# Rotating the first value tiles over three PSUM banks, moving the first head's mixes, and issuing two single residual loads ahead of large ones

## The chip, the cores and the metric

The kernel runs on one core of a Trainium2 chip. The metric is the device time of one execution in microseconds (us), as the median of several runs. Engines are named as the profile names them: PE is TensorE (PEld its weight loads), DVE is VectorE, ACT is ScalarE, POOL is GpSimd and SP is SyncE, which here only issues transfers. `L608` is line 608 of the kernel before.

## The reference

The input x has 2 sequences of 2048 positions with 256 features. First a recurrence is added to it, then an attention with experts (8 heads of width 64, 5 experts, 2 of them chosen for each position and head):

```python
x = x + rnn(layernorm(x))            # h = tanh(Wi x_t + bi + Wh h + bh), step after step
y = layernorm(x)
q, k = y @ Wq, y @ Wk                # per head, width 64
wv = topk_mask(y @ Ws, 2) * sigmoid(y @ Ws)      # gate of each expert
xv = einsum('btd,edk->btek', y, Wv)              # values of all 5 experts, no head in it
v  = einsum('bthe,btek->bhtk', wv, xv)           # a head's values: a weighted mix of experts
attn = softmax(q k^T / 8) v
mask_o = topk_mask(y @ Wd, 2)
x = x + einsum('bthe,bthk,ekd->btd', mask_o, attn, Wo)
```

The expert values xv are the same for all heads of a sequence. Only the mix v differs from head to head.

## The kernel before, in words

A first part, up to about 140 us, computes the recurrence in chunks and normalises. It isn't touched. It leaves x after the recurrence in DRAM as `x1d` (the residual that is added at the end) and its normalised transpose in SBUF as `xn2T`.

The attention works in 64 units: 16 heads (sequence by sequence, 8 each) by 4 blocks of 512 query positions. A unit has 4 steps, called T, and each step makes two score tiles: a tile has 128 key positions of two chunks by 512 queries (`scores`, L642). A tile goes through a pipeline that is LAG = 6 steps long:

- TensorE writes the scores in PSUM; ScalarE copies them to SBUF (`stage`, L654) and VectorE keeps a running maximum (`largest`, L664 to L670). Two score tiles fit in PSUM, so the second tile after waits for both.
- After a unit's eight tiles, TensorE transposes the maximum (`turn_max`, pm), VectorE reduces it (mq, L688), and TensorE spreads it over partitions (`spread_max`, pt, L697).
- The maximum is subtracted in SBUF (`subtract`, L710): on VectorE for a unit's first two tiles, on POOL for the other six. ScalarE takes the exponential (L713).
- TensorE multiplies with the head's values (`products`, L723, into o). POOL adds pairs of tiles with an accumulating DMA (`fold`, L735), and TensorE sums over the folded ones (`sums`, L744, into d).
- `take` (os, L759 and L760), `take_sums`, `weigh`, `masked` and `gather` bring a unit's output into `yd`, summed over heads; `turn_out` and `project_out` multiply with Wo (pz), add the residual z (L893) and store.

The values of the first sequence are made while the first head runs. `first_experts(c)` computes chunk c's values for all experts (tile pvf, 128 x 320 floats in PSUM, L581), ScalarE copies it to SBUF (xf, L608), and after each four chunks SyncE stores them for later heads. Tables of side work hold at which step it is issued: `first_experts(c)` stands behind step (c + 2) // 3, so chunk 0 at T=0, and chunks 13 to 15 at T=5. For the first head, `mix` multiplies four chunks by their gates on VectorE (wp, L624; L626), and `mix_sum` adds the five experts (L632). Within a step, `before` is issued ahead of the products, `between` after the tile copy and before the step's `largest`, and `behind` last.

[...] two buffers of a pool called misc (tiles pq, pk, pm, pt, wp, and others), one bank for o, one for d, and two score tiles of two banks each. In the drain, the scores' four banks serve other work.

The whole order is written out by hand (`with tc.manual_schedule()`): each engine executes its instructions in the order in which the program issues them, and waits at semaphores for what it needs. A transfer issued on SyncE waits in SyncE's queue as well.

After the last step, `drain()` finishes the last units: w, v and u are units 61, 62 and 63; tv and tu are the first tiles of v and u. The last outputs to be projected are numbered 0 to 15 in `outs`. The first four have a residual load each (`turn_out`, tag z, three buffers, 128 KB, L870), and the others come in blocks of four (`load_z`, 512 KB, L876). `fetch_y` (L810) reads a block of 640 KB from `yd`.

```python
z = yT_of.pop(("z", b, c), None)
if z is None:
    z = ap.tile([P, D], F32, tag="z", bufs=3, name=f"z{b}_{c}")
    nc.sync.dma_start(out=z, in_=x1d[c, :, b, :])
```

Of the kernel before, what the change touches and what calls it, by code (L numbers as in the profile page):

```python
# [8 lines left out]
F32 = mybir.dt.float32  # L9
# [5 lines left out]
P = 128  # L15
# [5 lines left out]
def pass_over(  # L21
# [17 lines left out]
    nc = tc.nc  # L39
    tc_pool, mark = tc.tile_pool, "s" if slow else ""  # L40

    def tile_pool(name, **kw):
        return tc_pool(name=name + mark, **kw)

    B, T, D = x.shape
    E, _, DH = Wv.shape
# [5 lines left out]
    NQ = T // QB  # L52
    QS = QB // P
# [17 lines left out]
    x1d = dram.tile([NCH, P, B, D], F32, name="x1d" + mark)  # L71
# [31 lines left out]
    for kc in range(KC):  # L103
        nc.sync.dma_start(
            out=wv[:, kc], in_=Wv[:, kc * P : (kc + 1) * P, :].rearrange("e p k -> p e k")
# [21 lines left out]
    def misc(shape, nm):  # L127
        return ps_m.tile(shape, F32, tag="m", name=nm)
# [148 lines left out]
    with tile_pool(name="prep", bufs=3) as pp, tile_pool(  # L277
        name="lna", bufs=3
    ) as lnp, tile_pool(name="ps_xi", bufs=3, space=PSUM) as ps_xi, tile_pool(
        name="ps_t", bufs=3, space=PSUM  # L280
# [286 lines left out]
    ap = ctx.enter_context(tile_pool(name="attn", bufs=2))  # L567
    four = ctx.enter_context(tile_pool(name="four", bufs=1))
    ps_o = ctx.enter_context(tile_pool(name="ps_o", bufs=1, space=PSUM))
# [7 lines left out]
    def by_quarters(dst, b, c, w):  # L577

        for kc in range(KC):
            for g in range(0, P, 32):  # L580
                nc.tensor.matmul(  # L581
                    dst[g : g + 32],
                    lhsT=xn2T[:, kc, b, c * P + g : c * P + g + 32],
                    rhs=w[:, kc],
                    start=kc == 0,
                    stop=kc == KC - 1,
                    tile_position=(0, g),
                )
# [9 lines left out]
    def first_experts(c):  # L598

        part = c // 4  # L600
        if c % 4 == 0:
            tag = ("y", "y", "xq", "pro")[part]
            xq_of[0, part] = four.tile([P, 4, DH, E], F32, tag=tag, bufs=1 + (tag == "y"), name=f"xf{part}")
        xq = xq_of[0, part]

        pv = ps_o.tile([P, E, DH], F32, tag="d", name=f"pvf{c}") if c % 2 else misc([P, E, DH], f"pvf{c}")
        by_quarters(pv.rearrange("p e k -> p (e k)"), 0, c, wv.rearrange("p c e k -> p c (e k)"))
        nc.scalar.copy(xq[:, c % 4], pv.rearrange("p e k -> p k e"))  # L608
        if c % 4 == 3:
            nc.sync.dma_start(out=xvd[0, part], in_=xq)  # L610
# [75 lines left out]
    def reduce_max(u):  # L686
        pm, mq = mx_of[u]
        nc.vector.tensor_reduce(mq, pm, AX.X, ALU.max)  # L688
# [23 lines left out]
    def exponential(t):  # L712
        nc.scalar.activation(ring[t], ring[t], AF.Exp)  # L713
# [91 lines left out]
    def fetch_y(u):  # L805

        i, n = units[u]
        b, _ = heads[i]
        y_of[b, n] = four.tile([P, QS, E, DH], F32, tag="y", bufs=2, name=f"y{b}_{n}")
        nc.sync.dma_start(out=y_of[b, n], in_=yd[b, n])  # L810
# [37 lines left out]
    yT_of = {"n": 0}  # L848
# [5 lines left out]
    def turn_out(b, c):  # L854
        yf = y_of[b, c // QS][:, c % QS].rearrange("p e k -> p (e k)")
        py = other(f"py{b}_{c}")[:, : len(o_chunks) * P] if spare else misc([P, len(o_chunks) * P], f"py{b}_{c}")
        py = py.rearrange("p (k n) -> p k n", n=P)
        for k, (r0, m) in enumerate(o_chunks):
            nc.tensor.transpose(py[0:m, k, :], yf[:, r0 : r0 + m], ident)
        yT = yT_all[yT_of["n"] % 2]  # L860
        yT_of["n"] += 1
        full = sum(m == P for _, m in o_chunks)
        nc.scalar.copy(yT[:, 0:full, :], py[:, 0:full, :])
        for k, (r0, m) in enumerate(o_chunks):
            if m < P:
                nc.scalar.copy(yT[0:m, k, :], py[0:m, k, :])
# [3 lines that stand above are left out]
            nc.sync.dma_start(out=z, in_=x1d[c, :, b, :])  # L870
        yT_of[b, c] = (yT, z)

    def load_z(b, n):

        z = ap.tile([P, QS, D], F32, tag="p1", bufs=RING[1], name=f"zz{b}_{n}")
        nc.sync.dma_start(out=z, in_=x1d[n * QS : (n + 1) * QS, :, b, :].rearrange("c p d -> p c d"))  # L876
        for s in range(QS):
            yT_of["z", b, n * QS + s] = z[:, s, :]
# [76 lines left out]
    before, between, first_behind, behind = {}, {}, {}, {}  # L955

    def at(table, T, f, *a):
        table.setdefault(T, []).append(lambda: f(*a))
# [9 lines left out]
    for i, (b, h) in enumerate(heads):  # L968
        T0 = i * H_T
        if i == 0:  # L970
            at(before, 0, keys, 0, 1)
            for c in range(NCH):
                at(behind, (c + 2) // 3, first_experts, c)
        else:

            at(before, T0 - 3 * U_T + 2, keys, i, 0)
            at(before, T0 - 2 * U_T + 2, queries, i, 0)
            at(before, T0 - U_T + 2, keys, i, 1)
        at(before, T0 + 2, queries, i, 1)
        for part in range(4):  # L980
            if i == 0:
                at(behind, (3, 5, 6, 7)[part], mix, i, part)
                at(behind, (3, 5, 6, 7)[part], mix_sum, i, part)
            else:
                T = T0 + U_T * (part - 2) + 2
                at(behind, T - 2, fetch, i, part)
                at(behind, T, mix, i, part)
                at(before, T + 1, mix_sum, i, part)
        if h == H - 3 and b + 1 < B:
            for c in range(NCH):  # L990
                T = T0 + c // 2 * U_T + 1
                at(before if c % 2 else behind, T + c % 2, experts, b + 1, c)
# [25 lines left out]
    for u, (i, n) in enumerate(units):  # L1018
        b, h = heads[i]
# [3 lines left out]
        outs = [(b, n * QS + s) for s in range(QS)]  # L1023
# [19 lines left out]
    def drain():  # L1043


        w, v, u = len(units) - 3, len(units) - 2, len(units) - 1
        tv, tu = HC * v, HC * u
        outs = [(B - 1, c) for c in range(NCH)]
        turned, projected = 2, 1

        def turn(n=1):
            nonlocal turned
            for _ in range(n):
                turn_out(*outs[turned])
                turned += 1

        def project(n=1):
            nonlocal projected
            for _ in range(n):
                project_out(*outs[projected])  # L1060
                projected += 1

        load_z(B - 1, NQ - 3)
        load_z(B - 1, NQ - 2)
        spread_max(v)
        turn_max(u)
        subtract(tv + 6, True)
        subtract(tv + 7)
        reduce_max(u)
        take_sums(w)  # L1070
        exponential(tv + 5)
        project()
        spread_max(u)
        products(tv + 4)
        products(tv + 5)
        fold(tv + 2)
        fold(tv + 4)
        exponential(tv + 6)
        exponential(tv + 7)
        subtract(tu, True)  # L1080
        close(w)
        gather(w)
        turn()
        exponential(tu)
        subtract(tu + 1, True)
        exponential(tu + 1)
        subtract(tu + 7)
        subtract(tu + 2, True)
        products(tv + 6)
        products(tv + 7)  # L1090
        fold(tv + 6)
        turn()
        fetch_y(v)
        project()
        load_z(B - 1, NQ - 1)
        take(v)
        sums(tv, tv + 2, True, False)
        exponential(tu + 2)
        subtract(tu + 3, True)
        exponential(tu + 3)  # L1100
        subtract(tu + 4, True)
        project()
        products(tu)
        products(tu + 1)
        turn()
        fold(tu)
        subtract(tu + 5, True)
        exponential(tu + 4)
        turn()
        project()  # L1110
        products(tu + 2)
        products(tu + 3)
        fold(tu + 2)
        sums(tv + 4, tv + 6, False, True)
        take_sums(v)
        exponential(tu + 5)
        subtract(tu + 6, True)
        turn()
        project()
        exponential(tu + 6)  # L1120
        products(tu + 4)
        products(tu + 5)
        exponential(tu + 7)
        turn()
        fetch_y(u)
        project()
        close(v)
        gather(v)
        products(tu + 6)
        products(tu + 7)  # L1130
        take(u)
        project()
        sums(tu, tu + 2, True, False)
        sums(tu + 4, tu + 5, False, False)
        sums(tu + 6, tu + 7, False, True)
        take_sums(u)
        turn()
        turn()
        project()
        turn()  # L1140
        project()
        turn()
        close_last(u, outs[-QS - 2 :])
# [117 lines left out]
```

## Time and profile before

| | us |
|---|---|
| median of 3 runs | 1560.38 (1559.92 to 1560.54) |
| profiled execution, its own time | 1562.38 |
| its span in the profile | 1560.5 |
| TensorE busy | 1513.2 |
| VectorE, ScalarE, POOL busy | 1300.0, 1245.4, 1287.0 |
| stretch of the first head, 143 to 192 | TensorE busy 41.97 of 49 |
| stretch of the drain, 1490 to 1561 | TensorE busy 59.62 of 71 |
| between them, 192 to 1490 | TensorE busy 1283.9 of 1298 |

The granted TensorE clock was 0.999 over the whole span and 0.96 in the last stretch. A row of an engine in order of time has the start, the duration, the operation with its line, output and inputs, how many instructions it joins, and in brackets how long the engine was idle before it and what ended that idle time. Matmuls overlap, so the duration of a group is less than the sum of its single matmuls.

### The profile page before, as it was taken

What the parts mean: (1) busy time and instruction counts of PE and PEld (TensorE: products, weight loads), DVE (VectorE), ACT (ScalarE), POOL (GpSimd) and SP (SyncE); (2) the same over time, 40 slices, a digit from 0 to 9 for tenths busy, and PEclk for the clock granted to TensorE, in tenths of its full rate; (3) what the DMA queues carried; (4) which work ended last, traced back from release to release, by engine and by line L of the source; (5) the groups of instructions that cost most, each with busy time, mean ns of one, the idle gap of its engine ahead of it and who ended that gap; (6) DMA issues with size and microseconds to landing.
All of it is one profiled execution on the core that took longest, in us unless ns stands there. A gap on an engine that the chain in (4) does not pass through costs nothing.

```text
span 1560.5 us, 41474 instructions
## 1 busy us (share of the span) xinstructions
PE 1513.2 (97%) x17582; PEld 534.4 (34%) x17582; DVE 1300.0 (83%) x1811; ACT 1245.4 (80%) x1617; POOL 1287.0 (82%) x855
## 2 busy tenths in 40 slices
PE   6999899999999999999999999999999999999988
PEld 5984222222233333333223332222222222222233
DVE  7474899999988877888987779999999999899873
ACT  4674688888888888888887778888888888888863
POOL 3154699999999987999997778899999999999970
PEclk9999999999999999999999999999999999999999
DMA  5021478888888887788786777888888888888963
GB/s 167 1 109 40 114 163 196 190 189 176 177 178 179 183 183 162 163 178 179 160 200 156 167 161 176 175 178 176 175 177 179 175 179 180 174 170 176 195 163 92
DMA packets 86821, 254.15 MB, mean 163 GB/s; under 512 B 11808, under 2 KB 31072, under 8 KB 86624
## 3 DMA queue, kind: packets, MB, share of 16 engines
q0 software_dynamic: 43488, 164.65, 57.9%
q1 hardware_dynamic: 41504, 86.13, 16.6%
q8 instruction: 140, 2.29, 0.6%
q10 hardware_dynamic: 1632, 0.61, 0.2%
q14 instruction: 57, 0.47, 0.1%
HBM read 59.46 MB, written 50.33 MB: 70 GB/s over the span
## 4 chain that ended last, share of the span: by engine, by line
PE 63%; DVE 19%; ACT 7%; issue 5%; DMA 3%; POOL 1%; ACTq 0%; SPq 0%; DVEq 0%; POOLq 0%
PE s L642 21%; PE o L723 17%; DVE m L664 11%; ACT p L654 5%; PE d L744 4%; DVE pro L789 3%; PE pq L166 3%; PE pk L147 3%; PE pz L885 2%; PE phb L368 2%; PE px L309 1%; PE pha L368 1%; DMA p<-p 1%; DMA z<-x1d 1%; ACT p L713 1%
## 5 line engine op out<-in xcount | busy, mean ns | idle before, releaser
L710 POOL TENSOR_TENSOR p<-p,top 128x1024 f32<-128x1024 f32 x378 | 1005.1, 2759 | 25.8 <-ACT top L703 25.5
L654 ACT COPY p<-s 128x1024 f32<-128x1024 f32 x512 | 511.5, 1012 | 139.6 <-issue 60.8
L713 ACT ACTIVATE p<-p 128x1024 f32<-128x1024 f32 x512 | 538.8, 1064 | 51.3 <-DVE p L710 42.7
L642 PE MATMUL s<-q,k 64*32 64x512 f32 x4096 | 501.6, 596 | 4.9 <-ACT p L654 2.5
L642 PE MATMUL s<-qs,k 64*32 64x512 f32 x4096 | 501.6, 596 | 3.5 <-ACT p L654 1.8
L723 PE MATMUL o<-p,v 128*32 128x512 f32 x4096 | 492.4, 598 | 5.1 <-DVE os L760 4.3
L664 DVE TENSOR_TENSOR m<-s,m 128x1024 f32<-128x1024 f32 x320 | 390.7, 1221 | 85.5 <-PE s L642 76.1
L735 POOL DMA_DIRECT2D p<-p x254 | 259.9, 1023 | 103.2 <-issue 43.7
L723 PEld LDWEIGHTS o<-p,v 128*32 128x32 f32 x4096 | 114.0, 109 | 301.5 <-issue 158.9
L642 PEld LDWEIGHTS s<-q,k 64*32 64x32 f32 x4096 | 100.5, 106 | 156.0 <-ACT p L654 60.3
L642 PEld LDWEIGHTS s<-qs,k 64*32 64x32 f32 x4096 | 100.4, 106 | 154.2 <-ACT p L654 58.1
L710 DVE TENSOR_TENSOR p<-p,pt 128x1024 f32<-128x1024 f32 x126 | 152.4, 1210 | 0.0
L744 PE MATMUL d<-p,ones 128*32 128x512 f32 x1032 | 136.3, 592 | 1.6 <-DMA p<-p 1.6
L664 DVE TENSOR_TENSOR m<-s,p 128x1024 f32<-128x1024 f32 x64 | 78.4, 1225 | 50.5 <-ACT p L654 49.6
L789 DVE TENSOR_TENSOR pro<-po,mr 128x1280 f32<-128x1280 f32 (+1 forms) x67 | 95.9, 1431 | 3.2 <-DVE mr L785 0.5
L626 DVE TENSOR_TENSOR xq<-xq,wp 128x1280 f32<-128x1280 f32 x60 | 89.2, 1487 | 2.1
L632 DVE TENSOR_REDUCE v<-xq 128x256 f32<-128x1280 f32 x60 | 88.5, 1475 | 0.0
L166 PE MATMUL pq<-xn2T,wq 128*32 128x512 f32 x512 | 62.2, 598 | 0.0
L147 PE MATMUL pk<-xn2T,wk 128*32 128x512 f32 x512 | 61.5, 598 | 0.0
L744 PEld LDWEIGHTS d<-p,ones 128*32 128x32 f32 x1032 | 34.0, 110 | 79.9 <-issue 76.0
L843 POOL DMA_DIRECT2D yd<-pro x48 | 60.1, 1252 | 0.0
L403 POOL TENSOR_TENSOR x<-x,hvb 128x512 f32<-128x512 f32 x14 | 17.8, 1275 | 45.8 <-ACT hs L376 34.2
(178 smaller groups left out, 1492.3 us busy)
## 6 DMA issues: line engine op xcount, KB each, us to landing
p<-p POOLq DMA_DIRECT2D x254, 512.0 KB, 5.4
xq<-xvd SPq DMA_DIRECT2D x60, 640.0 KB, 4.3
yd<-pro POOLq DMA_DIRECT2D x48, 640.0 KB, 6.5
qs<-q SPq DMA_DIRECT2D x64, 128.0 KB, 4.8
yd<-pro SPq DMA_DIRECT2D x8, 640.0 KB, 5.9
y<-yd SPq DMA_DIRECT2D x8, 640.0 KB, 8.2
x<-in_x SPq DMA_DIRECT2D x16, 256.0 KB, 5.8
x1d<-x SPq DMA_DIRECT2D x16, 256.0 KB, 2.0
```

Of the source, the lines that this page charges most:

```text
L147: nc.tensor.matmul(pk[at_col : at_col + 32], lhsT=wk[:, kc, h * DH + g : h * DH + g + 32], rhs=xc[:, kc, c0 // 2 : (c0 + HC) // 2, o, :], ...
L166: nc.tensor.matmul(pq[at_col : at_col + 32, :], lhsT=wq[:, kc, h * DH + g : h * DH + g + 32], rhs=xn2T[:, kc, b, n * QB : (n + 1) * QB], s ...
L626: nc.vector.tensor_tensor(xq, xq, wp.unsqueeze(2).to_broadcast([P, 4, DH, E]), ALU.mult)
L642: nc.tensor.matmul(ss[g : g + 32, o, :], lhsT=k_of[i][half, c, g : g + 32], rhs=q_of[i, n][o][half, :], start=True, stop=True, tile_positi ...
L654: nc.scalar.copy(p, ss)
L664: nc.vector.tensor_tensor(m, ss, ring[t - 1] if c == 1 else m, ALU.max)
L710: eng.tensor_tensor(p, p, top.unsqueeze(1).to_broadcast([P, 2, QB]), ALU.subtract)
L713: nc.scalar.activation(ring[t], ring[t], AF.Exp)
L723: nc.tensor.matmul(o_of[u][at_col : at_col + 32, :], lhsT=v_of[i][:, 2 * c + o, g : g + 32], rhs=ring[t][:, o, :], start=c == 0, stop=c == ...
L735: nc.gpsimd.dma_start(out=ring[t], in_=ring.pop(t + 1), accum_op=ALU.add)
L744: nc.tensor.matmul(den_of[u][32 * g : 32 * (g + 1), :], lhsT=ones32, rhs=ring[(t, t1)[g // 2]][:, g % 2, :], start=first, stop=last, tile_ ...
L789: nc.vector.tensor_tensor(dst, po[:, s : s + n, 0:DH].unsqueeze(2).to_broadcast([P, n, E, DH]), mr[:, s : s + n].unsqueeze(3).to_broadcast ...
```

## The change

It has three parts, and none adds or removes an instruction.

1. `first_experts`: the PSUM bank of pvf c. Before, odd c used the bank tagged d and even c a misc buffer. After, c mod 3 chooses: 0 misc, 1 bank o, 2 bank d.
2. First head: `mix` and `mix_sum` of the four parts stood together behind T = 3, 5, 6, 7. After, the mixes are issued behind T=2, between at T=4, and behind T=5 and T=6; the sums behind T=2, between at T=4, behind T=6, and between at T=8.
3. Drain: a new helper `load_z1` issues a single residual load. The loads of outputs 2 and 3 (z2, z3) come at the beginning of the drain, ahead of `load_z` of block 1 (zz1); before, they were issued by their `turn_out`, behind zz1 and zz2. `load_z` of block 2 (zz2) takes the place that block 3 (zz3) had, and block 3's comes after `fetch_y(u)`.

```diff
--- before.py
+++ after.py
@@ -603,7 +603,8 @@
             xq_of[0, part] = four.tile([P, 4, DH, E], F32, tag=tag, bufs=1 + (tag == "y"), name=f"xf{part}")
         xq = xq_of[0, part]
 
-        pv = ps_o.tile([P, E, DH], F32, tag="d", name=f"pvf{c}") if c % 2 else misc([P, E, DH], f"pvf{c}")
+        tag = (None, "o", "d")[c % 3]
+        pv = ps_o.tile([P, E, DH], F32, tag=tag, name=f"pvf{c}") if tag else misc([P, E, DH], f"pvf{c}")
         by_quarters(pv.rearrange("p e k -> p (e k)"), 0, c, wv.rearrange("p c e k -> p c (e k)"))
         nc.scalar.copy(xq[:, c % 4], pv.rearrange("p e k -> p k e"))
         if c % 4 == 3:
@@ -870,6 +871,10 @@
             nc.sync.dma_start(out=z, in_=x1d[c, :, b, :])
         yT_of[b, c] = (yT, z)
 
+    def load_z1(b, c):
+        yT_of["z", b, c] = ap.tile([P, D], F32, tag="z", bufs=3, name=f"z{b}_{c}")
+        nc.sync.dma_start(out=yT_of["z", b, c], in_=x1d[c, :, b, :])
+
     def load_z(b, n):
 
         z = ap.tile([P, QS, D], F32, tag="p1", bufs=RING[1], name=f"zz{b}_{n}")
@@ -979,8 +984,8 @@
         at(before, T0 + 2, queries, i, 1)
         for part in range(4):
             if i == 0:
-                at(behind, (3, 5, 6, 7)[part], mix, i, part)
-                at(behind, (3, 5, 6, 7)[part], mix_sum, i, part)
+                at(between if part == 1 else behind, (2, 4, 5, 6)[part], mix, i, part)
+                at(between if part % 2 else behind, (2, 4, 6, 8)[part], mix_sum, i, part)
             else:
                 T = T0 + U_T * (part - 2) + 2
                 at(behind, T - 2, fetch, i, part)
@@ -1060,8 +1065,9 @@
                 project_out(*outs[projected])
                 projected += 1
 
+        for o in outs[2:QS]:
+            load_z1(*o)
         load_z(B - 1, NQ - 3)
-        load_z(B - 1, NQ - 2)
         spread_max(v)
         turn_max(u)
         subtract(tv + 6, True)
@@ -1092,7 +1098,7 @@
         turn()
         fetch_y(v)
         project()
-        load_z(B - 1, NQ - 1)
+        load_z(B - 1, NQ - 2)
         take(v)
         sums(tv, tv + 2, True, False)
         exponential(tu + 2)
@@ -1123,6 +1129,7 @@
         exponential(tu + 7)
         turn()
         fetch_y(u)
+        load_z(B - 1, NQ - 1)
         project()
         close(v)
         gather(v)
```

## The prediction

> **What bounds the kernel now.** I read the page's busy shares first, then the chain that ended last, then each engine in order of time in the two stretches that the change touches.
>
> ```profile
> PE 1513.2 (97%) x17582; PEld 534.4 (34%) x17582; DVE 1300.0 (83%) x1811; ACT 1245.4 (80%) x1617; POOL 1287.0 (82%) x855
> ...
> PE 63%; DVE 19%; ACT 7%; issue 5%; DMA 3%; POOL 1%; ACTq 0%; SPq 0%; DVEq 0%; POOLq 0%
> ```
>
> TensorE is busy 97% of the span, so a gain can come only from its idle time. In the 50 us in which the first head starts, TensorE's records in order of time show it (start, duration, work, and in brackets the idle time before it and its releaser):
>
> ```profile
> 146.45 3.44 PE L581 MATMUL pvf<-wv,xn2T 128*32 128x320 f32 x48 [1.08 <-ACT q L176]
> ...
> 154.53 1.28 PE L581 MATMUL pvf<-wv,xn2T 128*32 128x320 f32 x16 [0.47 <-ACT xf L608]
> ...
> 159.15 0.62 PE L697 MATMUL pt<-ident,mq 128*128 128x128 f32 x4 [0.88 <-DVE mq L688]
> ...
> 168.93 1.28 PE L581 MATMUL pvf<-wv,xn2T 128*32 128x320 f32 x16 [1.63 <-ACT xf L608]
> ...
> 180.70 0.63 PE L642 MATMUL s<-q,k 64*32 64x512 f32 x4 [1.30 <-ACT p L654]
> ...
> 183.18 0.63 PE L683 MATMUL pm<-ident,mm 128*128 128x128 f32 x4 [0.53 <-DVE wp L624]
> ...
> 186.82 0.65 PE L697 MATMUL pt<-ident,mq 128*128 128x128 f32 x4 [1.16 <-DVE mq L688]
> ```
>
> Those seven idles sum to 7.05 us. Three are a value tile that waits for a PSUM bank; four go back to VectorE. VectorE in order of time, just ahead of the pt at 159.15:
>
> ```profile
> 155.13 0.17 DVE L624 COPY wp<-gates_all 128x20 f32<-128x20 f32 x1
> 155.34 1.49 DVE L626 TENSOR_TENSOR xf<-xf,wp 128x1280 f32<-128x1280 f32 x1
> 156.86 1.49 DVE L632 TENSOR_REDUCE v<-xf 128x256 f32<-128x1280 f32 x1
> 158.31 0.69 DVE L688 TENSOR_REDUCE mq<-pm 128x4 f32<-128x512 f32 x1
> ```
>
> A mix (0.17 + 1.49) and its sum (1.49) stand ahead of the row maximum mq. In the drain, the chain that ended last leaves TensorE:
>
> ```profile
> 1506.06 10.57 DMA z<-x1d
> ...
> 1516.72 0.25 DVE z L893
> 1516.97 0.20 issue
> 1517.18 0.70 DVE os L760
> 1517.88 0.14 issue
> 1518.02 3.27 PE o L723 x16
> ```
>
> A 128 KB residual, issued at 1506.06, lands 10.57 us later. VectorE's add waits for it and the take of the outputs (os) is behind the add on the same engine; TensorE's products behind that start after 2.03 us of idle and take 3.27 us, where the same 16 take 1.90 elsewhere. One more idle of TensorE nearby:
>
> ```profile
> 1513.63 0.62 PE L744 MATMUL d<-p,ones 128*32 128x512 f32 x2 [1.08 <-DMA p<-p]
> ```
>
> It is the fold of POOL issued at 1504.00, landed 9.6 us later. After 1518 TensorE has no gap over 0.2 us until 1554.3, and the execution ends at 1560.5.
>
> [...] the trace's 0.47 and 1.63 us are tile c waiting for tile c-2's copy out of one. [...] z1 (128 KB), issued at 1501.82 ahead of the large ones, landed in 2.6 us, z2 behind them in 10.6. [...] The 3.27 against 1.90 us fits a lowered clock[...].
>
> **Part 1, banks of the value tiles.** No work is added. Tile c goes to misc, o, d by c mod 3, so it needs tile c-3's copy and not c-2's; bank o is free until products(0), which come after pvf15. The waits at 146.45 (pvf4 in misc behind the query copy), 154.53 and 168.93 go: 1.08 + 0.47 + 1.63 = 3.18. A copy takes 0.43 and three tiles take 3.37 us of TensorE, so three banks cover it. The misc ring still holds pm, pt, wp; its two buffers now have fewer users.
>
> **Part 2, mix steps.** Same operations: four mixes and sums, 4 x 3.15 us of VectorE. Moved where VectorE idles (before 151.88 it had been idle 3.96, before 165.13 4.99). My walk, each instruction at the latest of its inputs:
> - Mix 0 with sum runs 147.95-151.15, delaying the maximum m7 by 0.5; tile s8 needs the copy of s7 (ends 153.41) at 153.92: margin 0.5.
> - Scores of T=4 start 153.92 (155.74 before); pt 157.2 (159.15), no mix ahead of mq now.
> - Mix 1 with sum, before T=4's maximum m9, 157.2-160.35: m9's end moves to 161.6, s11 needs its bank at 162.05: margin 0.45.
> - T=6's scores 166.37 (170.15): 3.8 gained. T=7's 171.95 (175.60).
> - VectorE is then full from 163.1 to 178.2, as it was from 165.13 to 187.9. That sets m15 at 174.85, its copy at 177.1, and s16 at 177.15 (180.70): 1.45 us of idle stays. Mix 3's sum, now before T=8's maximum, leaves mq1 earlier: pt1 at 181.45 (186.82), 0.85 idle between pm and pt1.
> - The stretch ends at 186.7 instead of 191.9: 5.2.
>
> Check: TensorE's work between 143.45 and 191.9 is 40.9 (pq 1.85, 12 value tiles at 1.12, seven pairs of scores at 1.88, pk 1.85, four pairs of products at 1.85, d 0.86, four transposes 2.3), so 7.5 is idle; 2.3 of it stays.
>
> POOL limits this. It is busy without a gap from 175.46, where its first fold waits for products(0,1), and that moves by 3.7 only. Its subtracts end 0.26-0.97 us ahead of the exponentials of the first three units (record by record, L710's end to L713's start), and a late exponential has 1.3 us of other products on TensorE as cover. So at least 3.7 + 0.26 = 4.0, at most 5.3; I take 4.9. From there units last 20.3 us in a loop of TensorE, ScalarE and VectorE, with 1.13 us of slack on POOL: the gain is carried along. The upper end needs the cover to hold, the lower end is the bare sum.
>
> **Part 3, drain.** No DMA is added; six change place. SyncE's order becomes z1, z2, z3, zz1, out z1, y2, out z2, zz2, out z3, two outs, y3, zz3. [...] z3 waits for out z0 (issued 1501.43, landed +2.7); zz1 stands behind it. z2 is issued about 1502.6 and lands, at 2.6-4.0 like its neighbours, about 1506; at its old 10.6 it would be 1513.2. Needed: 1512.11, when VectorE has done its pair of subtracts. z3 (issued from 1504.1, needed 1516.0) and zz1 (from about 1505, needed about 1519) have over 11 us. The later loads stay covered: VectorE first added zz2 at 1541.16 and POOL y2 at 1535.09; less the gain, 1536 and 1530, over 15 us from issue; zz3 and y3 come after these. With the add at 1512.11, os is 1512.98-1513.67. TensorE ahead of it still waits for the fold of 1504.00. I put its landing at 1512.6 instead of 1513.6, since one of the two 512 KB loads issued just before it has gone; the d and pz behind it then end about 1514.9 (2.36 after the landing, as before), and products(tu) run 1514.9-1516.85, where they ended at 1521.28. That is 4.4: 2.03 idle, 1.35 of slow clock, 1.0 of the fold's wait.
>
> What is late next: the last fold of unit tv. POOL issues it at 1515.13, behind gather(w) and a subtract that the change doesn't touch; it landed in 5.8 us, and zz2, issued about 1513 now, shares the engines. Estimate 6.5, so 1521.6. Its matmuls d, the second half of which reads it, began at 1525.61 and would begin at 1521.2, that half at 1521.7: nothing lost, gain 4.4. If it takes 9.7 us, as the one issued 1506.74 did, it lands at 1524.8 and the gain is 1.4. Best, with no fold late and os as the limit: 5.3.
>
> **Sum.** 4.9 + 4.4 = 9.3 us. The profiled execution took 1562.38, its span 1560.5; the median of runs, 1560.38, is equal to the span, so I take it as base: 1551.1 us.
>
> **Rivals.**
> - *POOL holds the head.* Cover on TensorE is not there: 4.0 from the head, 8.4 in all, 1552.0; with part of the drain lost 1553. For: POOL's slack of 0.26 us at unit 2. Chance 0.2.
> - *The fold takes z2's place.* zz2 slows the fold: 4.9 + 1.4, 1554.1. For: two of six folds took over 9 us while 512 and 640 KB loads ran; against: now only zz2 comes close to this one. Chance 0.17.
> - *The mixes re-stall.* Margins of 0.45-0.5 us fail at s8, s11 or s14: head 3, in all 7.4, 1553.0. Chance 0.12.
> - *Slower: cadence.* The head leaves POOL late, the loop settles on POOL's pace instead. Decides if POOL stays more than 2.4 us (slack 1.13 + cover 1.3) behind; 0.2 us on each of 55 units is 11 us: 1562. Against: POOL's lag is 1.5 by the walk, and units 28 and 29 came with 0.03 us of slack without a longer cadence. Chance 0.04.
> - *Nothing moves in the drain*: z2's 10.6 us was traffic, not its place. Even so it lands at 1513.2, costing at most 1.1: 1552.2. Chance 0.03.
>
> **How the numbers follow.** The forecast has 0.44; the rivals' cases 0.56. A measurement here tells 0.2%, 3.1 us, from no change. Range: below, both ends best (5.3 + 5.3): 1549.8, less 0.8 for a walk's error, 1549.0; above, 1556.0, fold and head both poor (3 + 1.4). All but the slower rival (0.04) and stacked losses (0.04, counted as same) are faster: 0.92, 0.04, 0.04.
>
> **What would show it.** Right: no wait for xf at L581; mq without a mix ahead; an idle of 1.4 at s16; the add z without a DMA wait, the 16 products after it near 1.9 us. Wrong: an ACT wait on POOL in units 1 to 3, a fold from 1515 landing after 9 us, a new idle at s8 or s11, or units other than 20.3 us apart.

## The result, and the profile after

The changed kernel took 1554.93 us in the median of 6 runs (1551.82 to 1556.47), the kernel before 1560.73 (1559.92 to 1561.83). The ratio is 0.9955, 95% interval 0.9945 to 0.9965: 7.0 us faster by the ratio, 5.8 by the medians. The forecast was 1551.1 in a range of 1549.0 to 1556.0. So the time lies in the range and the sign was right, but the likeliest sum, 9.3 us, was too large: by a third against the ratio, by more than half against the medians. The profiled execution took 1555.04 us, its span 1553.2.

First the busy shares of the changed kernel; the chain that ended last has the same shares as before.

```profile
PE 1512.4 (97%) x17582; PEld 533.9 (34%) x17582; DVE 1300.0 (84%) x1811; ACT 1246.0 (80%) x1617; POOL 1287.7 (83%) x855
...
PE 63%; DVE 19%; ACT 7%; issue 5%; DMA 3%; POOL 1%; ACTq 0%; SPq 0%; DVEq 0%; POOLq 0%
```

No work has gone; the span lost idle time. TensorE in order of time, 143 to 192 us, now has only two idles with a releaser, where there were seven (line numbers are one higher than before):

```profile
157.03 0.65 PE L698 MATMUL pt<-ident,mq 128*128 128x128 f32 x4 [0.79 <-DVE mq L689]
...
176.96 0.63 PE L643 MATMUL s<-q,k 64*32 64x512 f32 x4 [1.49 <-ACT p L655]
```

No value tile waits for a copy any more in this stretch. VectorE in order of time shows the moved mix: the row maximum mq comes first now, and the mix stands behind it.

```profile
156.29 0.69 DVE L689 TENSOR_REDUCE mq<-pm 128x4 f32<-128x512 f32 x1 [1.86 <-PE pm L684]
156.89 0.17 DVE L625 COPY wp<-gates_all 128x20 f32<-128x20 f32 x1
157.10 1.49 DVE L627 TENSOR_TENSOR xf<-xf,wp 128x1280 f32<-128x1280 f32 x1
158.62 1.49 DVE L633 TENSOR_REDUCE v<-xf 128x256 f32<-128x1280 f32 x1
```

In the drain, VectorE's add of z2 (at 1507.37) follows its subtracts with no wait. Two rows of TensorE and the chain that ended last show what is waited for now:

```profile
1508.62 0.62 PE L745 MATMUL d<-p,ones 128*32 128x512 f32 x2 [0.72 <-DMA p<-p]
...
1518.03 1.05 PE L745 MATMUL d<-p,ones 128*32 128x512 f32 x4 [0.30 <-DMA p<-p]
```

```profile
1499.35 9.22 DMA p<-p
...
1508.62 0.49 PE d L745
...
1510.32 0.19 PE o L724
1510.51 7.48 DMA p<-p
...
1518.03 1.05 PE d L745 x4
```

A fold took the residual's place in the chain, and then a later one, the fold of tile 6 of unit v (the last that v's sums read).

To say where the time went without the noise of the rest, I divided every profile at four events: the first copy of a score tile by ScalarE (L654), the first exponential of units 4 and 20, and the last copy of a score tile. "Head" is the time from the first copy to unit 4, "to 20" from the first copy to unit 20, "drain" from the start of the last copy to the end of the span, all in us. The last row is of runs that are told below.

| profile | first copy at | head | to 20 | drain | span |
|---|---|---|---|---|---|
| before | 129.00 | 124.65 | 461.16 | 61.46 | 1560.5 |
| changed | 128.93 | 120.40 | 456.75 | 58.86 | 1553.2 |
| gain | | 4.25 | 4.41 | 2.60 | 7.3 |
| before, five more with the old drain | 128.7 to 130.5 | | | 58.53 to 59.44 | |

### The profile page after: what moved, and what is told of

It is laid out like the page before. It is cut to its first block, busy times and chain, and to the rows that moved or that the text cites. A ratio compares the mean times of both kernels' runs of the same rounds, so it can differ in the third digit from the quotient of the medians.

```text
span 1553.2 us, 41472 instructions
## 1 busy us (share of the span) xinstructions
PE 1512.4 (97%) x17582; PEld 533.9 (34%) x17582; DVE 1300.0 (84%) x1811; ACT 1246.0 (80%) x1617; POOL 1287.7 (83%) x855
## 4 chain that ended last, share of the span: by engine, by line
PE 63%; DVE 19%; ACT 7%; issue 5%; DMA 3%; POOL 1%; ACTq 0%; SPq 0%; DVEq 0%; POOLq 0%
PE s L643 21%; PE o L724 17%; DVE m L665 11%; ACT p L655 5%; PE d L745 4%; DVE pro L790 4%; PE pq L166 3%; PE pk L147 3%; DMA p<-p 2%; PE pz L890 2%; PE phb L368 2%; PE px L309 1%; PE pha L368 1%; PE pv L581 1%; ACT p L714 1%
## 5 line engine op out<-in xcount | busy, mean ns | idle before, releaser
L736 POOL DMA_DIRECT2D p<-p x254 | 263.1, 1036 | 95.8 <-issue 42.3
L403 POOL TENSOR_TENSOR x<-x,hvb 128x512 f32<-128x512 f32 x14 | 17.9, 1276 | 45.8 <-ACT hs L376 34.2
```

The lines of the kernel that those rows point to most:

```text
L736: nc.gpsimd.dma_start(out=ring[t], in_=ring.pop(t + 1), accum_op=ALU.add)
```

## The experiments

Times are medians; a ratio is to the kernel before on the same chip, with its 95% interval.

**The head and the drain alone, and each kernel once more.** The first kernel leaves out the drain's edit (and its helper):

```diff
-        for o in outs[2:QS]:
-            load_z1(*o)
         load_z(B - 1, NQ - 3)
+        load_z(B - 1, NQ - 2)
...
-        load_z(B - 1, NQ - 2)
+        load_z(B - 1, NQ - 1)
...
-        load_z(B - 1, NQ - 1)
```

> Parts 1 and 2 alone (banks and mix steps), the drain as before. Theory A (the head gives the 4.65 us by which every late unit is shifted in the profile, and the drain's share in the medians is small): 4.6 us faster, about 1556.1. Rival B (the profile-to-profile reading is the true one; of a median gain of 5.8 the drain gives 2.9): 2.9 us faster, about 1557.8.

Measured: 1557.57 us, ratio 0.9967 (0.9956 to 0.9978), 5.2 us, near theory A's 4.6; B's 2.9 lies outside the interval (3.4 to 6.9). Head 120.32, drain 58.95. The second leaves out the head's edits (banks and mix steps as before):

```diff
-        tag = (None, "o", "d")[c % 3]
-        pv = ps_o.tile([P, E, DH], F32, tag=tag, name=f"pvf{c}") if tag else misc([P, E, DH], f"pvf{c}")
+        pv = ps_o.tile([P, E, DH], F32, tag="d", name=f"pvf{c}") if c % 2 else misc([P, E, DH], f"pvf{c}")
...
-                at(between if part == 1 else behind, (2, 4, 5, 6)[part], mix, i, part)
-                at(between if part % 2 else behind, (2, 4, 6, 8)[part], mix_sum, i, part)
+                at(behind, (3, 5, 6, 7)[part], mix, i, part)
+                at(behind, (3, 5, 6, 7)[part], mix_sum, i, part)
```

> Part 3 alone (the order of the residual loads), the head as before. Theory A: about 1.2 us faster, 1559.5, since the profiled execution of the kernel before was 2 us above the median of its runs and so its drain was a slow one. Rival B: 2.9 us faster, 1557.8. My prediction's own number was 4.4: 1556.3.

Measured: 1560.22 us, ratio 0.9986 (0.9979 to 0.9992), 2.2 us. Head 124.71, drain 58.42. The other two are the two kernels with no edit.

> The kernel before, unchanged, to have a second profiled execution of it and the spread between two sets of its runs. Theory A: the residual z2 lands sooner than the 10.6 us of the first profile, and the stretch from 1490 to the end is 1 to 2 us shorter. Rival B: it lands after 10 us again and the products behind it wait 2 us. Ratio 1.000 within 0.001.

Measured: 1561.47 us, ratio 0.9998 (0.9990 to 1.0006).

> The changed kernel, unchanged, for a second profiled execution and more runs. Both theories: about 5.8 us faster, 1554.9. Theory A: head again 4.65; the drain's end is set by the folds that the sums of unit tv read, and their landing (9.2 and 7.5 us in the first profile) differs by 1 us or more between the two executions, which makes its runs spread over 4.6 us. Rival: the folds land alike, and the spread comes from the middle units.

Measured: 1555.57 us, ratio 0.9961 (0.9949 to 0.9973).

The head's 5.2 and the drain's 2.2 add up to about the whole (7.0 by the ratio); 2.2 lies between the numbers of theories A and B, and its interval (1.2 to 3.3) reaches to both. My own 4.4 is outside. The second profile of the kernel before says why. TensorE in order of time there:

```profile
1517.90 1.92 PE L723 MATMUL o<-p,v 128*32 128x512 f32 x16 [1.92 <-DVE os L760]
1519.76 0.87 PE L859 MATMUL py<-ident,y 128*128 128x128 f32 x6
```

Theory A expected z2 to land sooner. It didn't: z2 was issued at 1506.32 and took 10.20 us, and the products had 1.92 us of idle ahead of them as before. But they took 1.92 us, not 3.27, and the six transposes 0.87, not 1.17. The drain was 59.44, 2.02 us shorter. A window laid over both profiles around these products (start and end of the window, its length, busy time of TensorE, its weight loads, VectorE, ScalarE and POOL, granted clock, DMA share, GB/s) has the clock. The profile I predicted from:

```profile
1518.00:1522.00 4.00, 3.98 (x20) 1.44 (x21) 3.72 (x4) 1.06 (x1) 0.86 (x1) 0.57 0.98 263
```

and the second one of the same kernel:

```profile
1517.00:1521.00 4.00, 2.91 (x26) 1.26 (x30) 3.94 (x6) 1.66 (x4) 0.86 (x1) 1.00 1.01 226
```

The clock fell to 0.57 in one and stayed at 1.00 in the other. Six profiles in all have the old drain, with idles of 1.9 to 2.0 us at this place; only the first one slowed. So the idle is regular, and the slow clock was seen in one of six. What the runs show of it stands in the last section.

The second profile of the changed kernel has a drain of 56.88 against 58.86. There the fold that the first d reads took 7.95 us instead of 9.22, and that of tile 6 5.83 instead of 7.48, and no fold is in the chain that ended last. Even so, the second half of the next d began only when the fold of tile 6 had landed, and d took 2.00 us instead of 1.04.

**Banks alone, mixes alone.** The first takes the changed line for `pv` only, the second the two lines with `mix` and `mix_sum` only (the diff above, read the other way).

> Part 1 alone (three banks for the value tiles), mixes and drain as before. Stretch from ScalarE's first copy of a score tile to the first exponential of unit 4: 124.66 us in both profiles of the kernel before, 120.42 with parts 1 and 2. Theory: the two bank waits ahead of VectorE's full stretch (1.08 + 0.47) are gained, the third (1.63) is not, since VectorE, full from there to 187.9, sets the later steps: 123.1, 1.5 us faster, about 1560.5. Rival: all three are gained, 121.5, 3.2 us.

Measured: 1559.65 us, ratio 0.9990 (0.9982 to 0.9998). Head 123.47: 1.2 us, near the theory's 1.5. The copies are no longer waited for, and VectorE, with its mixes at the old steps, sets the time: TensorE waits 1.60 us for mq ahead of pt, and 1.79 at s16.

> Part 2 alone (the first head's mixes at their new steps), banks and drain as before. Theory: the same stretch is 122.0, 2.7 us shorter, so that parts 1 and 2 add up to the 4.25 seen: of the bank waits that come back (3.18), 1.6 is hidden by VectorE's later limit. About 1559.3. Rival: the bank waits all come back in full and it is 123.6, 1.1 us shorter.

Measured: 1560.95 us, ratio 0.9998 (0.9990 to 1.0007). Head 125.23, which is 0.6 longer than before (0.3 at unit 20). Both expectations fell: neither had a new wait. TensorE in order of time has one in its second row:

```profile
158.78 0.65 PE L697 MATMUL pt<-ident,mq 128*128 128x128 f32 x4 [0.79 <-DVE mq L688]
160.44 3.44 PE L581 MATMUL pvf<-wv,xn2T 128*32 128x320 f32 x48 [1.02 <-DVE xf L626]
...
169.67 1.28 PE L581 MATMUL pvf<-wv,xn2T 128*32 128x320 f32 x16 [1.62 <-ACT xf L608]
```

VectorE there, ahead of 160.44:

```profile
158.64 0.17 DVE L624 COPY wp<-gates_all 128x20 f32<-128x20 f32 x1
158.90 1.49 DVE L626 TENSOR_TENSOR xf<-xf,wp 128x1280 f32<-128x1280 f32 x1
```

A mix puts its gates (wp) in a misc buffer, and holds it until the multiply ends. Moved to T=4, mix 1 holds the buffer that the next even value tile (pvf10) is to have. A second new wait comes in unit 1, where VectorE's `weigh` (mr) needs the mask of the output experts (`gates_all`, L254), which POOL works out beside its folds and subtracts:

```profile
208.48 0.18 DVE L785 TENSOR_TENSOR mr<-po,gates_all 128x20 f32<-128x20 f32 x1 [1.97 <-POOL gates_all L254]
```

In the kernel before, this mask was ready 0.3 us ahead of need:

```profile
208.22 0.18 DVE L785 TENSOR_TENSOR mr<-po,gates_all 128x20 f32<-128x20 f32 x1
```

The move is only harmless if the value tiles are elsewhere. To test that, the next kernel keeps the moved mixes and takes the value tiles out of misc, but with two banks:

```diff
-        pv = ps_o.tile([P, E, DH], F32, tag="d", name=f"pvf{c}") if c % 2 else misc([P, E, DH], f"pvf{c}")
+        pv = ps_o.tile([P, E, DH], F32, tag="d" if c % 2 else "o", name=f"pvf{c}")
```

> Part 2 (mix steps) with the value tiles in two banks and none in misc: even ones in bank o, odd ones in d; drain as before. From the first copy of a score tile to the first exponential of unit 4 the profiles had 124.7 us before, 125.2 with part 2 alone, 120.4 with parts 1 and 2. Theory (half of what part 2 lost is that a value tile in misc waits for pq and for a mix's gates wp, which VectorE holds until its multiply ends): the two misc waits, 1.07 and 1.02, go, the two for bank d (0.47, 1.62) stay: 123.1. Rival (only the depth of the rotation counts; with two banks tile c waits for tile c-2 everywhere): 124.5 or more, new waits for xf at even tiles.

Measured: 1559.85 us, ratio 0.9993 (0.9983 to 1.0002). Head 123.20, the theory's number. TensorE's rows:

```profile
153.53 1.28 PE L581 MATMUL pvf<-wv,xn2T 128*32 128x320 f32 x16 [0.68 <-ACT xf L608]
158.06 0.65 PE L697 MATMUL pt<-ident,mq 128*128 128x128 f32 x4 [0.79 <-DVE mq L688]
167.87 1.28 PE L581 MATMUL pvf<-wv,xn2T 128*32 128x320 f32 x16 [1.62 <-ACT xf L608]
```

Both misc waits are gone and both waits for a copy two tiles back stay. So of the 4.8 us between mixes alone (125.23) and mixes with three banks (120.40), leaving misc gives 2.0 and the third bank 2.8. The parts don't add: 1.2 and -0.6 alone, 4.25 together.

The profiles show where the gain goes. All times in this table are us after the first copy of a score tile; the last column is how long VectorE waits for the mask in unit 1:

| profile | first d | POOL's first fold | mask ready | unit 4 (head) | wait |
|---|---|---|---|---|---|
| before | 62.03 | 45.88 | 78.90 | 124.65 | none |
| banks alone | 60.81 | 42.84 | 77.67 | 123.47 | none |
| mixes alone | 60.72 | 46.90 | 79.73 | 125.23 | 1.97 |
| mixes, two banks | 58.73 | 44.91 | 77.73 | 123.20 | 1.69 |
| changed | 56.74 | 42.03 | 74.90 | 120.40 | 1.11 |

With the mixes alone, TensorE reaches the first d 1.3 us earlier, with the banks alone 1.2. But with the mixes alone POOL's first fold, which stands behind the first products, comes 1.0 later, the mask comes late with it, and unit 1 takes the gain back. In the three kernels with moved mixes the head follows the mask, and the mask follows POOL's first fold. That is read from traces; no run moved POOL's work alone.

**Which part of the drain's edit.** Here z2 and z3 stay ahead, and zz2 and zz3 go back to their old places:

```diff
         load_z(B - 1, NQ - 3)
+        load_z(B - 1, NQ - 2)
...
-        load_z(B - 1, NQ - 2)
+        load_z(B - 1, NQ - 1)
...
-        load_z(B - 1, NQ - 1)
```

> The changed kernel with zz2 and zz3 back at their old places, so that of part 3 only z2 and z3 ahead of zz1 is left. Theory (z2's landing was the wait, and zz2's place matters little): from ScalarE's last copy of a score tile to the end 57.0 to 58.5, no wait of VectorE's add on z2; the fold issued 5.0 us after that copy lands 9 us later or more, as zz2 runs beside it again, and d waits about 1 us for it; the fold of tile 6 lands in 5.5. Median as the changed kernel, 1555. Rival (part 3's gain is zz2's move): 59 or more, 1557.

Measured: 1555.89 us, ratio 0.9968 (0.9957 to 0.9980): nearly the ratio of the head alone (0.9967), and 1.5 us above the changed kernel on the same chip (below), though the two intervals overlap. The drain was 61.18. VectorE's add didn't wait for z2, but:

```profile
1514.55 1.90 PE L724 MATMUL o<-p,v 128*32 128x512 f32 x16
1516.26 1.03 PE L745 MATMUL d<-p,ones 128*32 128x512 f32 x4
1519.83 1.32 PE L745 MATMUL d<-p,ones 128*32 128x512 f32 x4 [2.54 <-DMA p<-p]
...
1521.91 2.46 PE L890 MATMUL pz<-wo,yT 128*32 128x256 f32 x24
```

The fold took 8.56 us, the wait reached 2.54, and the clock fell again (0.66 from 1520 to 1525 us; pz 2.46 instead of 1.50). My theory had this fold at 5.5 us and fell. This execution took 1558.14 us, the slowest of its eight and 2.25 above their median, so 61.18 isn't the drain of a usual run. What the profile does show is a way to lose: as soon as the outs are not held up by z2, SyncE comes sooner to the large load queued behind them. zz3 was issued 13.9 us after the last copy of a score tile, 18.6 in the first profile of the kernel before, and so it runs beside the fold, which is issued 16.2 us after that copy. The changed kernel has a large load at this very place too, zz2, and TensorE is idle for only 0.30 us there. What is more here is the early zz2, which was in flight until 17.9 us after that copy. So zz2's move is likely to be needed, but that isn't shown: the medians don't decide it.

**Can the fold's wait be taken away?** In the first of three versions both sums (d) are issued later, in the second zz1, y2 and zz2:

```diff
-        sums(tv, tv + 2, True, False)
...
-        sums(tv + 4, tv + 6, False, True)
-        take_sums(v)
         exponential(tu + 5)
         subtract(tu + 6, True)
         turn()
         project()
+        sums(tv, tv + 2, True, False)
+        sums(tv + 4, tv + 6, False, True)
+        take_sums(v)
```

> The changed kernel with both sums of unit tv's folds (d) and the take of them moved behind the second next output's projection, so that no fold is waited for where TensorE has other work. From ScalarE's last copy of a score tile to the end the profiles had 58.9, 56.9 and 58.4 us with the new drain, 61.5, 59.4 and 59.0 with the old one. Theory A (the landing of the folds now sets the drain's length and its spread): 55.5 to 56.5, 1.5 us faster than the changed kernel in the median, about 1553.5, no idle of TensorE before d. Rival: the work after it waits for the later d (close of v), and nothing is gained: 58, 1555.3.

Measured: 1553.75 us (1552.26 to 1554.19), ratio 0.9951 (0.9939 to 0.9964), drain 56.67, no idle of TensorE before d. In this execution the folds took 7.82 and 5.72 us, though, where also the unedited changed kernel had a drain of 56.88.

```diff
         for o in outs[2:QS]:
             load_z1(*o)
-        load_z(B - 1, NQ - 3)
...
         turn()
-        fetch_y(v)
         project()
-        load_z(B - 1, NQ - 2)
+        load_z(B - 1, NQ - 3)
...
         turn()
+        fetch_y(v)
+        load_z(B - 1, NQ - 2)
         fold(tu)
```

> The changed kernel with the loads of block 1 (zz1), of y2 and of block 2 (zz2) issued one step later each, so that no large load of SyncE runs beside the folds issued 5.0 and 7.7 us after ScalarE's last copy of a score tile. Theory F (the large loads slow those folds): the first lands within 6.5 us instead of 8.0 to 9.2, and d doesn't wait for it. Rival G (the two folds slow each other): 8 us or more again. In both, zz1 and zz2 meet the fold of tile 6, which takes 7.5 us or more, so no gain in the median is expected: 1555 to 1556.

Measured: 1553.87 us (1551.96 to 1555.42), ratio 0.9955 (0.9943 to 0.9967), drain 56.52. The first fold took 6.79 us and the second 6.82, where the three profiles of the changed kernel have 7.95 to 9.43 and 8.93 to 9.68 for them: the large loads cost those folds 1 us or more each, as theory F has it, though it expected 6.5. The fold of tile 6 took 4.59, not over 7.5, since zz1 landed 1.4 us after this fold's issue and y2 was issued 2.0 us after it. TensorE waited for no fold.

> The changed kernel with the late sums of e5 and the late loads of e7 together. Theory A (what is left in the drain is TensorE's own work): 56.5 us from the last copy of a score tile to the end, as with either alone, and the median 1 to 1.5 us below the changed kernel on the same chip, since no execution can have the late-fold drain of 58.9. Rival (a late y2 or zz stalls the later outputs): 57.5 or more, no gain.

Measured, with both edits: 1553.80 us (1552.81 to 1554.98), ratio 0.9954 (0.9940 to 0.9969), drain 56.66, as with either alone. With no fold waited for, TensorE's work is the drain's length. And the changed kernel on the same chip:

> The changed kernel again, on the same chip as the two versions of its drain. Theory A: the drain 56.9 or 58.9 us, as the fold of tile 6 lands in 5.8 or 7.5; head 4.3 to 4.5 as before; 6.1 to 7.0 us faster than the kernel before.

Measured: 1554.40 us (1553.38 to 1556.15), ratio 0.9958 (0.9944 to 0.9972), drain 58.44, with the fold of tile 6 at 7.46 us.

The three versions' medians lie 0.5 to 1.8 us under the changed kernel's three (1554.40 to 1555.57), partly on other chips. Each shortens the drain by about 2 us where the changed kernel has the slow folds (58.44, 58.86) and by 0.2 to 0.4 where it doesn't (56.88). The intervals of the ratios overlap, so no version is shown to be faster than the changed kernel.

## Why the prediction was right, and where it wasn't

**What bounds the kernel, and the sign**: right. TensorE's idle time was the only thing to gain, at the two places named.

**Part 1 and part 2, the walk**: right nearly to the instruction. Forecast pt at 157.2, measured 157.03; s16 at 177.15, measured 176.96 with 1.49 of idle for the 1.45 forecast; pt1 at 181.45, measured 181.29. Only one small idle stands elsewhere: 0.79 us stayed ahead of pt, and the 0.85 forecast ahead of pt1 didn't come. TensorE reached the first d at 185.66 instead of 191.02, 5.36 us earlier for the 5.2 forecast. The margins of 0.45 to 0.5 held, so the rival "the mixes re-stall" didn't come.

**POOL limits this**: right in kind, with another wait than the one priced. POOL's first fold moved from 175.46 to 171.53, by 3.9. The forecast looked at the exponentials, which wait for POOL's subtracts, and gave a late one 1.3 us of cover. That wait is 0.2 to 0.3 us in unit 1 and is missing in the profile of the head alone, whose head is as short (120.32). What takes the gain is VectorE's wait for the mask of the output experts, which POOL delivers and which the forecast didn't have. In the changed kernel it is

```profile
203.86 0.18 DVE L786 TENSOR_TENSOR mr<-po,gates_all 128x20 f32<-128x20 f32 x1 [1.11 <-POOL gates_all L254]
```

and TensorE, behind VectorE's maximum and ScalarE's copy, then has the idle that follows from it:

```profile
207.84 0.63 PE L643 MATMUL s<-qs,k 64*32 64x512 f32 x4 [1.03 <-ACT p L655]
```

The eight profiles with both parts all have this wait, 1.02 to 1.14 us. Unit 1 began 5.3 us earlier, and of that 4.2 to 4.35 was left at unit 4, and 4.4 to 4.7 at unit 20 (461.16 and 461.20 before; 456.54 to 456.80 in the eight). I took 4.9; the rival "POOL holds the head", with 4.0 and a chance of 0.2, was nearer. The slower rival didn't come: each later unit took the same time in both kernels within 0.5 us. But "20.3 us" is true only of some: units 11 to 34 took 20.4 to 27.9 in the kernel before, and units 28 and 29, which the prediction named as proof, 21.09 and 20.45.

**The step that failed: part 3's "2.03 idle, 1.35 of slow clock, 1.0 of the fold's wait".** Three terms were off.
- The 1.35 us of slow clock belonged to that one execution. In the five other profiles with the old drain it wasn't there (products 1.92 us at a granted clock of 1.00). I also took the profiled execution for a typical one, because its span (1560.5) equalled the median of the runs. But a run's own time is 1.8 to 1.9 above its span here (1562.38 against 1560.5; 1555.04 against 1553.2). So that execution was 2.0 us above the median, its drain was 2.02 longer than the second profile's, and what I counted as a gain had to be taken from a base that didn't have the loss. The sum should have been made with the products at 1.90, as elsewhere.
- The fold issued at 1504.00 was to take 8.6 us and took 9.22, 7.95 and 9.43 in three profiles of the changed kernel. Counted from the last copy of a score tile it landed after 13.9 us in the mean, with the old drain (six profiles) as with the new one (four). So the 1.0 us was nothing.
- "Nothing lost" at the last fold of tv: it was to take 6.5 and took 7.48, 5.83 and 7.46. The two d of four matmuls, 1.04 us in the second profile of the kernel before, end 2.37 after the first one's start in the changed kernel (1516.71 to 1519.08), and 2.00 to 2.35 in the other three profiles with the new drain. That is 1.2 us lost in the mean.

What stays of the sum is the 2.0 us of idle less that 1.2, so 0.8 us.

Without the slow clock the old drain is 58.5 to 59.4 us, 59.1 in the mean of five profiles; the new one 58.86, 56.88, 58.44 and, alone, 58.42, in the mean 58.15. That is about 0.9 us, or 1.3 with the one slow execution counted in. With the head's 4.5 it makes 5.4 to 5.8, which is what the medians gave (5.8), and near the lower end of the ratio's interval. By ratios the drain alone gave 2.2 (1.2 to 3.3), and the changed kernel 7.0, 6.1 and 6.6 in its three sets of runs, so up to 1 us is not accounted for. The rival "the fold takes z2's place", with its 1.4 us from the drain, came nearest, and should have had the larger chance; but the fold took 7.5 us at most in the changed kernel, not the 9.7 that the rival had. The text that zz2 alone would come close to this fold was true, and enough: in the singles-only profile, with one large load more in flight, it took 8.56 and was waited for 2.54 us, and in the late-loads profile, with the large loads mostly away from it, it took 4.59.

**DMA queue order**: z2 and z3, now ahead of the large loads, landed in 2.54 and 2.03 us instead of 10.57 and 9.47; for z2 the forecast was 2.6 to 4.0. zz1, which took 4.04 before, landed in 11.47 now, beside two folds. The order among SyncE's loads isn't all of it, since z2 now also goes ahead of both folds: a 128 KB output that is issued between them, 6.63 us after the last copy of a score tile, took 8.97 us before and still 5.46 in the late-loads profile, which has no large load there. The rival "nothing moves in the drain", with z2 late in any place, didn't come.

**Range**: it held, with the measured time in its upper half, where the rivals of POOL and of the fold had put it. That is in part luck: by the profiles the drain gave less than its poor end of 1.4, and the head, well above its own of 3, made up for it.

## What to carry to other kernels

Before a gain is summed from one profile, compare that execution's own time with the median of the runs in the same measure, and price a slow stretch at the duration that the same instructions have elsewhere. When an engine is nearly full, follow everything that it delivers, not only its largest work: here a small result of POOL, the mask of the output experts, took back 1 us of 5.3. When a wait at the head of a queue goes, what stands behind it in that queue can start earlier too (in the singles-only profile zz3 was issued 13.9 us after the last copy of a score tile instead of 18.6): ask what those transfers will then run beside. Two edits that share a buffer ring may be worth nothing alone and much together (here 1.2 and -0.6 us alone, 4.25 together), so cost them in combination, and look at how long each tenant holds its buffer.

## What the runs showed of the hardware that was not expected

The granted TensorE clock fell after an idle of about 2 us in some executions and not in others. Of seven profiles with an idle of 1.9 us or more of TensorE in the drain, two had it: the first of the kernel before (products 3.27 us) and the singles-only one (pz 2.46 us). In both the mean from 1515 to 1525 us was 0.83, in the five others 1.00. In the first profile of the kernel before the clock was 0.50 from 1518.45 to 1521.86, and 1.00 ahead of that from 1505 and behind it to 1555. The length of the idle alone doesn't tell the executions apart: that profile had 2.03 us, and the profiles of the banks alone, the mixes alone and the two banks had 2.03 to 2.04 at the same place, and their products took 1.92 us at 1.00. In the profile of the head alone, too, with an idle of 1.96, the clock was 1.00 from 1505 to 1525. What decides whether the clock falls isn't shown.

The clock differs between executions near the start as well, which no edit touches. In four of fourteen profiles the clock is 0.83 from 20 to 30 us, and the first copy of a score tile comes at 130.3 to 130.6 us. In the ten others it is 1.00, and the copy comes at 128.7 to 129.1. All four profiles are of kernels with both parts of the head's change; that this is more than chance isn't shown. The stretch from 20 to 30 us for the kernel before:

```profile
20.00:30.00 10.00, 8.02 (x42) 6.60 (x42) 8.84 (x47) 5.33 (x11) 3.44 (x7) 1.00 0.40 102
```

and for the head alone:

```profile
20.00:30.00 10.00, 7.99 (x33) 6.32 (x33) 8.84 (x46) 4.12 (x8) 3.36 (x7) 0.83 0.43 116
```

That is 1.5 us of a run's spread. Another 3 us lie between units 30 and 34, which took 107.65 to 110.69 us in these profiles without regard to the edit; what sets that is open, so the spread of the changed kernel's runs (1551.82 to 1556.47) is only partly explained by its folds.
